# Second feed-forward matrix of a decoder block: 26 block products in place of 28

## The chip, the cores and the metric

One core of one Trainium2 chip runs the whole kernel. The metric is the device time of one execution in microseconds (us). The core has a matrix engine (PE, with its weight loads shown as PEld), a vector engine (DVE), an engine for activation functions (ACT), a general engine (POOL) and an engine that here only issues transfers (SP). Each engine takes its own instructions in the order in which the built program has them.

## What is computed

A decoder block on x of shape (4, 2048, 512): three layer norms, each followed by a sub-block that is added to x. The first is a linear recurrence over the four rows of the leading axis, the second is attention over 77 rows of context, and the third is a feed-forward block. Cut to what matters:

```python
x = x + recurrence(layernorm(x))
x = x + attention(layernorm(x), ctx) @ Wo.T          # softmax over 77 keys, 16 heads
h = layernorm(x) @ W_exp + b_exp                     # 512 -> 2048
h = gelu(butterfly(h, up_weights) + up_bias)
y = butterfly(h, down_weights) @ W_con + b_con       # 2048 -> 512
x = x + y + down_bias
```

A butterfly is linear, so butterfly and dense matrix are folded on the chip into one matrix, once per execution: a first matrix of 512 x 2048 and a second of 2048 x 512. All is in float32.

## The kernel before

**Units.** The 2048 positions are cut into 16 units of 128. A unit holds 128 positions of each of the four rows t. For each unit the kernel runs two programs side by side: `feed_forward` of unit u, and `front` of unit u+1 (first two sub-blocks and the third norm). `front` is a generator with some 50 stopping points. `feed_forward` calls `step()` after a fixed number of matmuls, and `step()` advances `front` in proportion. This gives the program order; a scheduler then sets the order on each engine from its own estimates of durations, and that order is fixed in the built program.

**Prologue.** Before the first unit, `_prepare` folds the two matrices on the chip and writes them to DRAM together with the sums of blocks that the fast products need: `up7` for the first matrix, `dn7` for the second. The front of unit 0 is mixed into it. The prologue's large buffers `wup` and `wdn` give their room to the buffers of the main loop.

**Fast block products.** Both matrices are applied by Winograd's form of Strassen's scheme: two by two blocks with seven products in place of eight. For the second matrix the left side is the activations (rows t in two halves, hidden features in two halves) and the right side is the matrix (hidden features in two halves, output features in two halves). Counted in blocks a quarter as long (one row t, a quarter of the hidden features), the seven products are 28.

**First matrix (up phase), L665.** Hidden features are taken in eight pairs p of 128. A pair has seven up products of two matmuls each, spread over `up_head(p)`, `up_tail(p-1)` and `up_mid(p)`; each matmul is 128x128 by 128x256. The right sides are blocks of the normed x (`xnt`) and four sums of them, `tb`, made by `combine` (L633 to L636). The results pass from PSUM through DVE and ACT's gelu (L670) into activations a11, a12, a21, a22 of each pair. The last gelu of the last pair, in `up_tail(7)`, makes a21. POOL then makes two sums per pair (L711, L712).

**Second matrix (down phase), L736.** `down(i)` takes seven products of 16 matmuls, one load of 1 MiB each (`w_dn`, in three rotating buffers shared with `w_up`). POOL changes the sums s of all eight pairs twice between them (L746, L753). Results are added into the residual `xt` by DVE, and by POOL for the sum u2d that goes to three places (L755).

**What stands in `front` meanwhile.** For each row t: scores on PE (L562), maximum and subtraction on DVE (L566, L567), exponential on ACT (L568), sum and reciprocal on DVE (L570, L571), the multiplication by the reciprocal on POOL (L572, 128x1232), then transposes on PE (L584), copies to SBUF by ACT and DVE (L587, L589) and the context products (L594). ACT loads a table whenever it changes between exponential and gelu. After the four rows come the output product (L504 with `ps_w`), the sums `sw` on POOL and DVE (L603 to L606), three additions on POOL (L617), and the third norm (statistics L425 on DVE, rows L451, transposes L460).

Of the kernel before, what the change touches and what calls it, by code (L numbers as in the profile page):

```python
# [23 lines left out]
NB = HID // P  # L24
NU = B // P
HC = D + 1
LOW = 7
HIGH = 4
LN_EPS = 1e-5
MAGIC = 12582912.0  # L30


# [192 lines left out]
def _prepare(nc, keep, pool, room, late, banks, dram, ident, wexp_t, up_low, up_high, up_bias, dn_low, dn_high, wcon,  # L225
             wup, wdn, bias, up7, dn7):

# [122 lines left out]
    for c in range(NC):  # L350
        for g in range(4):
# [5 lines left out]
            yield  # L357
    h = NB // 2
    order = [r * h + b for b in range(h) for r in range(2)]

    def turned(b):
        ps = banks()
        for c in range(NC):
            nc.tensor.transpose(ps[:, c * P : (c + 1) * P], wup[:, c, b * P : (b + 1) * P], ident)
        evict(t[:, b, :], ps)

    share[0] = 6
    for n in range(2):
        turned(order[n])
    for n, b in enumerate(order):  # L370
        if n + 2 < NB:
            turned(order[n + 2])
        ps = banks()
        nc.tensor.matmul(ps, lhsT=el[:, b, :], rhs=t[:, b, :], start=True, stop=True)
        evict(wdn[:, b, :], ps)
        if n == h:
            nc.sync.dma_start(out=b1, in_=brow[1, :].rearrange("(b p) -> p b", p=P))
        if n % 4 == 3:
            f = slice(n // 4 * 2, n // 4 * 2 + 2)
            b11, b12, b21, b22 = (wdn[:, r * h + f.start : r * h + f.stop, c * (D // 2) : (c + 1) * (D // 2)]  # L380
                                  for r in range(2) for c in range(2))
            t1, t2, t3, n4 = (wup[:, i, :].rearrange("p (x y) -> p x y", x=2)[:, :, f.start * P : f.stop * P] for i in range(4))
            nc.vector.tensor_tensor(t1, b12, b11, ALU.subtract)
            nc.gpsimd.tensor_tensor(t3, b22, b12, ALU.subtract)
            nc.vector.tensor_tensor(t2, b22, t1, ALU.subtract)
            nc.gpsimd.tensor_tensor(n4, b21, t2, ALU.subtract)
            for i, w in ((0, b11), (1, b21), (2, b22), (4, t1), (6, t3), (5, t2), (3, n4)):
                nc.sync.dma_start(out=dn7[i][:, f, :], in_=w)
        yield
# [5 lines left out]
def kernel(ctx: ExitStack, tc: tile.TileContext, x, ctx_t, ssm_vec, ssm_vt, ssm_vinv, wq_t, wk_t, wv_t,  # L395
# [231 lines left out]
    def combine(xnt, res):  # L627


        b11, b12, b21, b22 = (xnt[:, c : c + 2, t : t + 2, :] for c in (0, 2) for t in (0, 2))  # L630
        tb = ffn.tile([P, 4, 2, 2, P], F32, tag="tb", bufs=1, name="tb")
        t1, t2, t3, n4 = (tb[:, i] for i in range(4))
        nc.vector.tensor_tensor(t1, b12, b11, ALU.subtract)  # L633
        nc.gpsimd.tensor_tensor(t3, b22, b12, ALU.subtract)
        nc.vector.tensor_tensor(t2, b22, t1, ALU.subtract)
        nc.gpsimd.tensor_tensor(n4, b21, t2, ALU.subtract)  # L636
        res.append((b11, b21, b22, n4, t1, t2, t3))

    def feed_forward(u, xt, rhs, other):
# [4 lines left out]


        slot = [0]
        lead = 0 if u else 8

        def step():
            slot[0] += 1  # L650
            past = slot[0] - lead
            for _ in range(max(past, 0) * 50 // (102 - lead) - max(past - 1, 0) * 50 // (102 - lead)):
                next(other, None)
# [5 lines left out]
        act = []  # L659
        live = {}  # L660

        def up(p, i, ps, first):
# [9 lines left out]
        def up_head(p):  # L672
            if early:
                w = early.pop()
            else:
                w = weights([P, 7, 2, P], "w_up")
                nc.sync.dma_start(out=w, in_=up7[p])
# [11 lines left out]
        def up_mid(p):  # L689
            w, a, b, c, p1, u2 = live[p]  # L690
            up(p, 2, a, False)
            a11, a12, a21, a22, s1 = (acts.tile([P, 2, P], F32, tag=g, name=g)
                                      for g in ("a11", "a12", "a21", "a22", "s1"))
            gelu(a11, a, p)
# [4 lines left out]
            gelu(a22, a22, h + p)  # L699
            act.append((a11, a12, a21, a22, s1))  # L700

        def up_tail(p):
            w, a, b, c, p1, u2 = live[p]
            a11, a12, a21, a22, s1 = act[p]
            up(p, 4, b, False)
            nc.vector.tensor_tensor(a12, b, p1, ALU.add)  # L706
            gelu(a12, a12, h + p)
            up(p, 3, c, False)
            nc.vector.tensor_tensor(a21, c, u2, ALU.add)
            gelu(a21, a21, p)  # L710
            nc.gpsimd.tensor_tensor(s1, a21, a22, ALU.add)  # L711
            nc.gpsimd.tensor_tensor(a21, a11, a21, ALU.subtract)  # L712
            del live[p]

        for p in range(h):
            with tc.manual_schedule(engines={mybir.EngineType.PE}) if u == 0 and p < 4 else nullcontext():
# [3 lines left out]
                up_mid(p)  # L720
            if p == 1 and u + 2 < NU:
                xts[u + 2] = load_x(u + 2)
            r, d = xt[:, p // 2, p % 2 * (D // 2) : (p % 2 + 1) * (D // 2)], slice(p % 2 * (D // 2), (p % 2 + 1) * (D // 2))
            nc.gpsimd.tensor_tensor(r, r, ybias[:, d], ALU.add)  # L724
        up_tail(h - 1)

        a, b, c, b7, a4 = (bank(g).rearrange("p (t d) -> p t d", t=2) for g in "abcba")
        lhs = {1: 0, 2: 1, 3: 4, 4: 3, 5: 4, 6: 4, 7: 2}
        r11, r12, r21, r22 = (xt[:, t : t + 2, d : d + D // 2] for t in (0, 2) for d in (0, D // 2))

        def down(i, ps, first):
            w = weights([P, h, D // 2], "w_dn")
            nc.sync.dma_start(out=w, in_=dn7[i - 1])
            for p in range(h):
                for t in range(2):
                    nc.tensor.matmul(ps[:, t, :], lhsT=act[p][lhs[i]][:, t, :], rhs=w[:, p, :],  # L736
                                     start=first and p == 0 and t == 0, stop=p == h - 1, skip_group_check=True)
                step()

        def store(t, d, r):  # L740
            nc.sync.dma_start(out=out[t : t + 2, u * P : (u + 1) * P, d : d + D // 2].rearrange("t p d -> p t d"), in_=r)

        down(5, c, True)
        nc.vector.tensor_tensor(r22, c, r22, ALU.add)
        for p in range(h):
            nc.gpsimd.tensor_tensor(act[p][4], act[p][4], act[p][0], ALU.subtract)  # L746
        down(1, a, True)
        u2 = acts.tile([P, 2, D // 2], F32, tag="u2d", bufs=1, name="u2d")
        nc.scalar.copy(u2, a)
        down(6, b, True)  # L750
        nc.vector.tensor_tensor(u2, b, u2, ALU.add)
        for p in range(h):
            nc.gpsimd.tensor_tensor(act[p][4], act[p][1], act[p][4], ALU.subtract)  # L753
        for r in (r12, r22, r21):
            nc.gpsimd.tensor_tensor(r, r, u2, ALU.add)  # L755
        down(2, a, False)
        nc.vector.tensor_tensor(r11, a, r11, ALU.add)
        store(0, 0, r11)
        down(7, b7, True)
        nc.vector.tensor_tensor(r22, b7, r22, ALU.add)  # L760
        store(2, D // 2, r22)
        nc.vector.tensor_tensor(r21, b7, r21, ALU.add)
        down(4, a4, True)
        nc.vector.tensor_tensor(r21, a4, r21, ALU.add)
        store(2, 0, r21)
        down(3, c, False)
        nc.vector.tensor_tensor(r12, c, r12, ALU.add)
        store(0, D // 2, r12)
        for _ in other:
# [10 lines left out]
    wq7 = dram.tile([P, 7, NC // 2, D // 2], F32, name="wq7")  # L780
    dn7 = [dram.tile([P, NB // 2, D // 2], F32, name=f"dn7_{i}") for i in range(7)]
    xts = {}
# [3 lines left out]
    with ExitStack() as stack, tc.manual_schedule(engines={E.PE, E.SP, E.Pool}):  # L786
# [6 lines left out]
        prep = _prepare(nc, tc.keep_in_program_order, pool, rooms, lambda: xpool.tile([P, NB, P], F32, tag="xt1", name="bd"),  # L793
                        banks, dram, ident, wexp_t, up_low, up_high, up_bias, dn_low, dn_high, wcon, wup, wdn, hbias, up7, dn7)
        room = (work.tile([P, NC, T * NK], F32, tag="pr", name="ct"), xpool.tile([P, NC, D], F32, tag="xt1", name="wk"),
# [34 lines left out]
        for n, _ in enumerate(prep):  # L830
# [8 lines left out]
            if n == 24:  # L839
                xts[1] = load_x(1)  # L840
            if n == 17:
                early.append(work.tile([P, 7, 2, P], F32, tag="pt", bufs=1, name="w_first"))
# [7 lines left out]
    xlast = ctx.enter_context(tc.tile_pool(name="xlast", bufs=1, reuse_waits="tile"))  # L850
    acts = ctx.enter_context(tc.tile_pool(name="acts", bufs=NB // 2, reuse_waits="tile"))
    wts = [ctx.enter_context(tc.tile_pool(name=f"wts{i}", bufs=1, reuse_waits="tile")) for i in range(2)]
# [4 lines left out]
    def weights(shape, name):  # L857
        loaded[0] += 1
        return wts[loaded[0] % 3 - 2].tile(shape, F32, tag="w", name=name)

    combine(ready[0][2], ready)
    for u in range(NU):
# [73 lines left out]
```

## Time and profile before

| what | us |
|---|---|
| median of 3 runs | 2628.69 (2628.46 to 2633.15) |
| the profiled execution's own time | 2630.88 |
| its span | 2629.1 |
| second matrix on PE, L736, four groups of the page's table | 373.7 + 248.6 + 125.0 + 113.3 busy |
| first matrix on PE, L665, larger groups | 395.5 + 261.9 + 131.7 + 130.4 busy |
| POOL: small sums of activations L711, L712, L746, L753 | 93.1 + 98.1 + 92.9 + 97.3 |
| POOL: normalisation L572, 64 times | 143.9, 2249 ns each |
| one table load on ACT | 1283 ns, 122 of them in the two groups |
| load of w_dn, 1 MiB, from issue to landing | 4.8 (median) |

A page's line of a group gives the source line, the engine, the operation, the tiles out and in, how many, the busy time and the mean of one; after the bar stands the idle time of the engine before it and what ended it. Matmuls in float32 appear as two records each. Durations of matmuls overlap, so the price of one is read from the distance of starts.

### The profile page before, as it was taken

How to read it: one execution, taken by the hardware profiler on the slowest of the kernel's cores; microseconds unless marked ns; L12 is line 12 of the kernel's file. 1: busy time of each engine (PE TensorE's matmuls, PEld its weight loads, DVE VectorE, ACT ScalarE, POOL GpSimd, SP SyncE). 2: the span in 40 equal slices, each digit the busy share in tenths (PEclk: the TensorE clock that was granted, in tenths of full speed). 3: DMA queues.
4: the chain of work that ended last, by engine and by line, in shares of the span. 5: the costliest groups of instructions: out<-in, count | busy, mean ns of one | idle time of the engine just before them, and what ended most of it. 6: DMA issues, size and time to landing. Idle time of an engine off the chain costs nothing.

```text
span 2629.1 us, 37413 instructions
## 1 busy us (share of the span) xinstructions
PE 2565.7 (98%) x14536; PEld 2180.5 (83%) x14536; DVE 1442.7 (55%) x3333; ACT 811.4 (31%) x1472; POOL 962.0 (37%) x1045
## 2 busy tenths in 40 slices
PE   8898999999999999999999999999999999999999
PEld 5766788888888888888888888888888888888888
DVE  6665546545554654565456455645645554554541
ACT  2342414133241413324141332414124241413420
POOL 4533333415233341523435152342515234252523
PEclk9998999999999999999999999999999999999999
DMA  5735233342423334252332424233242424323243
GB/s 178 255 94 201 81 127 126 105 148 82 173 95 120 133 102 150 82 174 94 121 132 92 147 95 166 90 134 132 87 150 97 160 93 136 132 87 135 96 134 139
DMA packets 95106, 333.60 MB, mean 127 GB/s; under 512 B 15313, under 2 KB 49233, under 8 KB 77777
## 3 DMA queue, kind: packets, MB, share of 16 engines
q1 hardware_dynamic: 94930, 331.21, 36.2%
q8 instruction: 116, 1.90, 0.3%
q14 instruction: 60, 0.49, 0.1%
HBM read 297.61 MB, written 33.57 MB: 126 GB/s over the span
## 4 chain that ended last, share of the span: by engine, by line
PE 86%; DVE 7%; ACT 4%; issue 1%; POOL 1%; DMA 0%; SPq 0%; ACTq 0%; DVEq 0%; POOLq 0%
PE ps_a L736 13%; PE ps_b L665 10%; PE ps_b L736 8%; PE ps_w L504 7%; PE ps_q L504 7%; PE ps_c L665 7%; PE ps_a L665 7%; PE ps_c L736 7%; PE ps_sc L562 5%; PE ps_pt L584 4%; PE ps_s L519 3%; PE ps_o L594 2%; PE ps_t L460 2%; ACT L568 1%; DVE st L425 1%
## 5 line engine op out<-in xcount | busy, mean ns | idle before, releaser
L665 PE MATMUL ps_b<-tb,w_up 128*128 128x256 f32 x1524 | 395.5, 380 | 0.0
L736 PE MATMUL ps_a<-w_dn,a 128*128 128x256 f32 x1536 | 373.7, 380 | 0.0
L711 POOL TENSOR_TENSOR s<-a,a 128x256 f32<-128x256 f32 x128 | 93.1, 727 | 681.9 <-ACT a L670 459.5
L665 PEld LDWEIGHTS ps_b<-tb,w_up 128*128 128x128 f32 x1524 | 286.1, 191 | 39.4
L670 ACT ACTIVATE a<-a,hbias 128x256 f32<-128x256 f32 x384 | 193.8, 508 | 404.8 <-DVE a L706 276.7
L736 PEld LDWEIGHTS ps_a<-w_dn,a 128*128 128x128 f32 x1536 | 282.4, 190 | 41.6 <-issue 2.8
L665 PE MATMUL ps_a<-xnt,w_up 128*128 128x256 f32 x1016 | 261.9, 380 | 5.5 <-DMA w_up<-up 5.5
L736 PE MATMUL ps_c<-w_dn,s 128*128 128x256 f32 x1024 | 248.6, 379 | 1.2 <-POOL s L711 1.2
L461 ACT COPY xnt<-ps_t 128x512 f32<-128x512 f32 x128 | 73.6, 588 | 515.7 <-PE ps_t L460 515.7
L572 POOL TENSOR_TENSOR pr<-pr,sm 128x1232 f32<-128x1232 f32 x64 | 143.9, 2249 | 242.4 <-DVE sm L571 232.8
L665 PEld LDWEIGHTS ps_a<-xnt,w_up 128*128 128x128 f32 x1016 | 190.1, 191 | 31.2 <-DMA w_up<-up 5.9
L736 PEld LDWEIGHTS ps_c<-w_dn,s 128*128 128x128 f32 x1024 | 188.8, 190 | 29.4 <-POOL s L711 1.6
L612 DVE TENSOR_TENSOR xt<-ps_w,xt 128x512 f32<-128x512 f32 x96 | 66.2, 689 | 212.0 <-PE ps_w L504 145.8
L724 POOL TENSOR_TENSOR xt<-xt,ybias 128x256 f32<-128x256 f32 x128 | 99.3, 810 | 223.5 <-DVE xn L451 223.5
L562 PE MATMUL ps_sc<-kbd,qt 128*128 128x308 f32 x512 | 172.8, 435 | 7.4 <-DVE pr L567 6.7
L584 PE MATMUL ps_pt<-ident,pr 128*77 128x128 f32 x1024 | 144.2, 276 | 8.7 <-DVE pt L589 3.3
L568 ACT ACTIVATE pr<-pr 128x308 f32<-128x308 f32 x256 | 111.3, 457 | 132.8 <-DVE pr L567 132.2
L584 PEld LDWEIGHTS ps_pt<-ident,pr 128*77 128x77 f32 x1024 | 117.5, 147 | 41.2 <-ACT pt L587 10.3
L504 PE MATMUL ps_q<-xnt,wq 128*128 128x256 f32 x640 | 151.1, 379 | 0.0
L504 PEld LDWEIGHTS ps_q<-xnt,wq 128*128 128x128 f32 x640 | 121.4, 190 | 16.8 <-issue 0.3
L682 ACT COPY p<-ps_a 128x256 f32<-128x256 f32 x128 | 47.7, 373 | 272.8 <-PE ps_a L665 272.8
L665 PE MATMUL ps_c<-tb,w_up 128*128 128x256 f32 x508 | 131.7, 382 | 0.0
(207 smaller groups left out, 4600.8 us busy)
## 6 DMA issues: line engine op xcount, KB each, us to landing
w_dn<-dn SPq DMA_DIRECT2D x112, 1024.0 KB, 4.8
w_up<-up SPq DMA_DIRECT2D x127, 896.0 KB, 4.5
wq<-wq SPq DMA_DIRECT2D x16, 1792.0 KB, 8.4
xt<-in_x SPq DMA_DIRECT2D x16, 1024.0 KB, 5.4
out<-xt SPq DMA_DIRECT2D x64, 256.0 KB, 4.7
wdn<-in_wexp_t SPq DMA_DIRECT2D x4, 1024.0 KB, 10.2
wdn<-in_wcon SPq DMA_DIRECT2D x4, 1024.0 KB, 5.0
up<-wo SPq DMA_DIRECT2D x8, 512.0 KB, 2.8
```

What stands on the lines that cost most here:

```text
L461: nc.scalar.copy(xnt[:, :, t, :], ps)
L504: nc.tensor.matmul(tiles[key][:, r, :], lhsT=lhs(i, r, k), rhs=rhs(i, r, k), start=key == i and r == 0 and k == 0, stop=k == 1, skip_group ...
L519: nc.tensor.matmul(ps[:, 2 * i : T, f * NS : (f + 1) * NS], lhsT=xpt[:, i, c * (P // NS) + f, :], rhs=gt[:, 0 : T - 2 * i, :], start=i == ...
L562: nc.tensor.matmul(ps[:, 0 : 4 * NK], lhsT=qt[:, g, t, :], rhs=kbd[:, t, g, :], start=True, stop=True)
L568: nc.scalar.activation(pg, pg, AF.Exp, scale=1.0 / math.sqrt(DH))
L572: nc.gpsimd.tensor_tensor(pr, pr, sm.unsqueeze(2).to_broadcast([P, NH, NK]), ALU.mult)
L584: nc.tensor.transpose(pt_ps[0:NK, j, :], pr[:, 4 * g + j, :], ident)
L665: nc.tensor.matmul(ps, lhsT=w[:, c, :], rhs=rhs[i - 1][:, c], start=first and c == 0, stop=c == 1, skip_group_check=True)
L670: nc.scalar.activation(out, x, AF.Gelu, bias=hbias[:, b : b + 1])
L711: nc.gpsimd.tensor_tensor(s1, a21, a22, ALU.add)
L724: nc.gpsimd.tensor_tensor(r, r, ybias[:, d], ALU.add)
L736: nc.tensor.matmul(ps[:, t, :], lhsT=act[p][lhs[i]][:, t, :], rhs=w[:, p, :], start=first and p == 0 and t == 0, stop=p == h - 1, skip_gro ...
```

## The change

The second matrix is applied by 26 products of blocks. The left side is 16 blocks, named a(t)(k): row t, quarter k of the hidden features. The right side is eight blocks, b(k)(d): quarter k, half d of the outputs. Each product multiplies one left block or sum of left blocks by one right block or sum of right blocks, with four matmuls, and its result is added to one to four places of the output.

```diff
+FIRST = 0, NB // 2, NB // 4, 3 * NB // 4
+SUMS = {name: (x, op, y) for name, x, op, y in (line.split() for line in """d0 a13 - a03
+e a03 - a23
+f a30 - a31
+g a32 - a31
+h a10 - a00
+i a22 - a02
+n6 d0 - a12
+n7 a11 - h
...
+l24 m24 + n8""".splitlines())}
+LEFT = "l0 a11 l2 l3 e n7 l6 n11 n8 l9 n9 a00 f l13 l14 l15 n10 n6 a21 d0 g l21 l22 l23 l24 a02".split()
+DOWN = ((11, "x", "+01"), (12, "y", "+30"), (25, "w", "+00"), (5, "x", "+00"), (16, "y", "+31"), (3, "v", "+20"),
+        (14, "x", "+10"), (15, "y", "+21"), (7, "w", "+20"), (20, "z", "+31"), (1, "x", "+11"), (18, "y", "+20"),
...
```

`SUMS` has 28 sums of left blocks, each one POOL instruction of 128x512. `LEFT` names each product's left side and `DOWN` gives the order of the products: number, PSUM sum it goes to, and places (sign, row t, half d). `_down_plan` puts the sums four products ahead of their user and gives each a place: five blocks of its own (x0 to x4), the four blocks of `tb` up to product 17, and blocks a(t)2 and a(t)3 once nothing reads them any more.

```diff
+        if not isinstance(v, int):
+            fits = [p for p in free if (p[1] not in lent or last[v][1] <= until) and (n >= early or p[1] in own)]
+            best = min(fits, key=lambda p: (p[0], p[1] not in lent))
+            free.remove(best)
+            place[v] = best[1]
```

In the plan the order on POOL after the first four sums is: a23 - a20, then g = a32 - a31, i = a22 - a02, n9 = a12 - g, and so on. In the scheduled program of a unit in the steady state POOL has after a23 - a20 and g six more sums, the third normalisation, five sums, the fourth normalisation.

In the prologue all 16 blocks are transposed first, then multiplied; after every fourth one, 17 sums and one negated sum of right blocks of 128x256 are made, ten on DVE and eight on POOL, and written by two transfers; six plain blocks are written at the end:

```diff
+            for lot in RIGHT:
...
+                for i, (name, x, op, y) in enumerate(lot):
+                    made[name] = w[:, i, :]
+                    if op == "n":
+                        nc.vector.scalar_tensor_tensor(made[name], made[x], -1.0, made[y], ALU.mult, ALU.subtract)
+                        continue
+                    engine = nc.vector if name in ("24", "5", "1", "8", "14", "2", "20", "10", "22") else nc.gpsimd
+                    engine.tensor_tensor(made[name], made[x], made[y], ALU.add if op == "+" else ALU.subtract)
+                nc.sync.dma_start(out=dn26[SLOT[lot[0][0]] : SLOT[lot[0][0]] + len(lot), :, j, :].rearrange("s p d -> p s d"), in_=w)
```

In `feed_forward` the pace of `front` is set to the new number of steps, the activations go into four buffers `quarter` that hold all rows of a quarter, four sums are made in the second half of the up phase, and the down phase follows the plan. Weights come in pairs of blocks, 512 KiB each:

```diff
-            for _ in range(max(past, 0) * 50 // (102 - lead) - max(past - 1, 0) * 50 // (102 - lead)):
+            for _ in range(max(past, 0) * 50 // (98 - lead) - max(past - 1, 0) * 50 // (98 - lead)):
...
-            nc.gpsimd.tensor_tensor(s1, a21, a22, ALU.add)
-            nc.gpsimd.tensor_tensor(a21, a11, a21, ALU.subtract)
...
+            if p >= h // 2:
+                made(*plan.pop(0)[1:])
...
+        for kind, where, *rest in plan:
+            if kind == "sum":
+                made(where, *rest)
+                continue
+            i, name, goes = DOWN[rest[0]]
+            n = rest[0] % 2
+            if not n:
+                pair = weights([P, 2, NB // 4, D // 2], "w_dn")
+            nc.sync.dma_start(out=pair[:, n], in_=dn26[SLOT[str(i)]])
...
+            ps, left = sums[name], place(where)
+            for j in range(NB // 4):
+                nc.tensor.matmul(ps, lhsT=left[:, j, :], rhs=pair[:, n, j, :], start=first and j == 0, stop=j == NB // 4 - 1,
+                                 skip_group_check=True)
+                if j % 2:
+                    step()
...
+                if to[0][0] == "+":
+                    nc.vector.tensor_tensor(r, x, r, ALU.add)
+                else:
+                    nc.vector.tensor_tensor(r, r, x, ALU.subtract)
...
+            if i == 6:
+                store(3, slice(0, D // 2))
+        store(3, slice(D // 2, D))
```

A second `w_up` block is loaded ahead in the prologue, into the room of `qt`, and in unit 0 the load of x for unit 2 moves from p = 1 to p = 6:

```diff
-            if p == 1 and u + 2 < NU:
+            if p == (1 if u else 6) and u + 2 < NU:
...
+            if n == 28:
+                early.append(work.tile([P, 7, 2, P], F32, tag="qt", bufs=1, name="w_second"))
+                nc.sync.dma_start(out=early[1], in_=up7[1])
```

## The prediction

> **What bounds the kernel now.** I read the page first: one engine is nearly full, and the chain that ended last is almost all its own.
>
> ```profile
> span 2629.1 us, 37413 instructions
> ...
> PE 2565.7 (98%) x14536; PEld 2180.5 (83%) x14536; DVE 1442.7 (55%) x3333; ACT 811.4 (31%) x1472; POOL 962.0 (37%) x1045
> ...
> PE 86%; DVE 7%; ACT 4%; issue 1%; POOL 1%; DMA 0%; SPq 0%; ACTq 0%; DVEq 0%; POOLq 0%
> ```
>
> Then the windows, cut at the end of each unit's last product. The columns are length, then busy time of PE, PEld, DVE, ACT and POOL, then clock and DMA.
>
> ```profile
> 819.44:973.45 154.01, 152.68 (x865) 130.54 (x865) 85.54 (x199) 48.41 (x88) 55.50 (x58) 1.00 0.36 122
> 973.45:1127.45 154.00, 152.67 (x865) 130.52 (x865) 85.64 (x199) 48.40 (x88) 55.52 (x58) 1.00 0.35 122
> ```
>
> A unit repeats every 154.00 us and PE is idle for 1.33 of them. So PE work taken out counts in full, and so does any new wait of PE. Last, the timelines of one unit (start, duration, engine, line): PE, then POOL, then ACT.
>
> ```profile
> 914.22 0.63 PE L584 MATMUL ps_pt<-ident,pr 128*77 128x128 f32 x4 [0.36 <-ACT a L670]
> ...
> 930.21 1.04 PE L584 MATMUL ps_pt<-ident,pr 128*77 128x128 f32 x8
> ...
> 951.94 1.89 PE L736 MATMUL ps_a<-w_dn,a 128*128 128x256 f32 x8
> 953.66 1.89 PE L504 MATMUL ps_w<-wo,sw 128*128 128x256 f32 x8
> ```
>
> ```profile
> 905.19 2.25 POOL L572 TENSOR_TENSOR pr<-pr,sm 128x1232 f32<-128x1232 f32 x1 [8.86 <-DVE sm L571]
> ...
> 923.88 2.25 POOL L572 TENSOR_TENSOR pr<-pr,sm 128x1232 f32<-128x1232 f32 x1
> ...
> 941.52 1.27 POOL L603 TENSOR_TENSOR sw<-ot 128x512 f32<-128x512 f32 x1 [1.04 <-DVE ot L596]
> 942.74 1.27 POOL L605 TENSOR_TENSOR sw<-ot 128x512 f32<-128x512 f32 x1
> ...
> 947.70 3.72 POOL L617 TENSOR_TENSOR xt<-xt,w 128x512 f32<-128x512 f32 x3
> ```
>
> ```profile
> 908.09 1.28 ACT L670 ACT_TABLE_LOAD   x1
> 909.38 0.51 ACT L670 ACTIVATE a<-a,hbias 128x256 f32<-128x256 f32 x1
> ```
>
> Prices from these. Eight PE records (four matmuls of 256 columns) take 1.73 us, so 0.432 each. A POOL sum of 128x512 follows the last after 1.22 to 1.24 us; I use 1.23. A normalisation of probabilities (L572) takes 2.25. Here its third instance ends at 926.1 and PE reads it at 930.21: 4 us in hand.
>
> [...] POOL stood 8.86 us before L572 with sums queued behind. [...] The trace shows 1.28 and the next ACTIVATE 0.01 later, no drain; I use 1.29. [...]
>
> **The change part by part.** Order of instructions in the changed program is known, so positions on PE can be added up from prices: 0.432 for a 256-column matmul, 0.52 for scores (308 columns), 0.43 for four transposes, 1.01 for sixteen context matmuls. Time zero is the unit's first up matmul. On the unit before, the same addition from the first scores to 930.21 gives 31.96 of the 33.20 seen; 0.36 is the wait shown, so switches cost 0.9 on that stretch.
>
> 1. Matmuls. 112 of the second matrix become 104: 8 x 0.432 = 3.46 us a unit, 16 units: -55.3.
>
> 2. POOL sums. Removed: 32 small ones (L711, L712, L746, L753: 0.73 to 0.78 each, 23.8 us) and three of L755 (3.8). Added: 28 x 1.27 = 35.5. POOL goes from 55.5 to about 63.4 us of 150: no average problem. The order is. The sum g (a32 - a31) needs the last gelu of the up phase. Behind it in POOL's queue stand six more sums, then the third normalisation, five sums, and the fourth.
>  - When g can start: the last up product ends on PE at 78.8, with switches 79.1. DVE has the result by 79.8, but ACT's queue first holds the gelu of a12 (done 78.3), a table load, two exponentials, a load back: 78.3 + 1.3 + 0.8 + 1.3 = 81.7, then the gelu 0.5: g starts at about 82.3.
>  - Third normalisation ends at 82.3 + 7 x 1.23 + 2.25 = 93.2. PE reaches its transposes at 90.75 + 0.7 = 91.5: it waits 1.7.
>  - Fourth ends at 82.3 + 12 x 1.23 + 2 x 2.25 = 101.6. PE's place is 96.1 + 1.1 = 97.2, so the total wait is 4.3 (taking 0.1 off for overlap of starts). Everything on PE is queued behind, down products included, though their sums are ready.
>  Not shown by the old trace; bounds: without the table loads g starts no earlier than 80.2, leaving 2.3[...]. I take 4.3, in the 15 units with a next front: +64.5.
>
> 3. Other sums. Later ones sit on blocks already read: they wait for a PE product that is four or more products before their user (l6 waits for product 17 of the order, counting from 0, and is used in 23): hidden; if not, up to 1 us.
>
> 4. First softmax. DVE now takes a maximum of the next batch row ahead of the first row's sum (L570): probabilities ready near 72.5 against PE's 71.7: 0.7 x 15 = +10.5 (bounds 0 and 1.2).
>
> 5. Evictions. Seven of 128x512 (0.63 to 0.69 us) become 25, mostly 128x256 at about 0.42: some +7 us of DVE a unit, 92 of 150. Hidden, except before the third norm: there four evictions share 7.8 us with the statistics and PE waits about 0.7 instead of 0.16: +0.55 x 15 = +8 (bounds 0 and 1.5).
>
> 6. The 0.36 wait of PE shown above goes: the bank it needed is copied in time in the new order: -5.4.
>
> 7. Weights. 7 loads of 1 MiB become 26 of half that: 13 MiB a unit, always two in flight per buffer of three. The tightest place is the end of the phase, where a pair is used up in 8 x 0.432 = 3.46 us. Two other pairs cover 6.9 us; a 1 MiB load lands after 4.8. Hidden, with 2 us in hand. SP has 20 more issues; the stores and the x load stand behind the weights as before. If that cover goes: rival C.
>
> 8. Prologue. The right sums grow from 4 to 18 half-width ones per round, in four rounds: eight on POOL, 8 x 0.8 = 6.4 us a round, so POOL ends near 183.7 + 25.6 = 209 and the first up phase's own POOL sum near 211; before, PE stood until 212.88 for w_up (5.46). Two up blocks are preloaded, so PE then has 12 up products against 5, but w_up for the third waits behind about 4.5 MB of stores, until 225 to 230. I take +5 (bounds -3 and +18).
>
> 9. The last unit has no front and no wait of item 2; it ends on a smaller eviction and store (-0.5) and pulls its weights fastest (+1): +0.5.
>
> Sum on the span: -55.3 + 64.5 + 10.5 + 8 - 5.4 + 5 + 0.5 = +27.8, so 2629.1 becomes 2656.9. The profiled execution took 2630.88, 1.8 outside the span, and the median of runs is 2.2 below it: 2656.5, say 2657.
>
> **Rivals.**
> A. POOL is never late. For: its busy share is under half, and PE has other down products to issue. Against: PE issues in order, and the twelve sums and two normalisations are 19.3 us of queue against about 18.1 of PE. Then -55.3 and +5 of prologue: 2578.
> B. The wait is there, but small. This is the main case's own sum on the other side of the line: g starts at 80.2 because ACT does the gelu before the exponentials' loads, and items 4 and 5 are nothing. Per unit -3.46 + 2.3 - 0.36 = -1.5; 15 units, the last one's -3 and the prologue: -20.5, so 2608. It decides once g starts by about 81.4, where the wait equals the 3.46.
> C. Slower still: weights. Busy DMA share gives 331.21 MB / (0.362 x 2629.1 us) = 348 GB/s at full engines, 3.0 us per MiB; but the busiest slice of the page moved only 255, or 4.1. Then a pair falls 0.65 behind in each of some 7, 4.5 less 1.9 in hand = 2.6 us a unit, on top of the main case: 2657 + 42 = 2699.
> That 26 products are not what is run is excluded: PE's order has 104 matmuls.
>
> **How the numbers follow.** Main 0.57 (own range 2634 to 2688: wait from 3.4 to 5.0, prologue from -3 to 18), A 0.14, B 0.15, C 0.14. A change under 0.2% (5.3 us) can't be told from none; 0.04 of the main and B cases lies there. So faster 0.27, same 0.04, slower 0.69. Range 2600 to 2700: A lies below it, a worse C above.
>
> **What would show it.** A third and fourth L572 that end after PE is free, a wait of 1 to 2 us and one of 2 to 3 us of PE transposes on POOL in each unit, and a unit of 155 to 156.5 us, show item 2. A unit near 150.5 with no such wait shows A. PE waiting for w_dn shows C. Units equal among themselves and a first stretch longer by over 15 us would put the loss in item 8. If ACT's gelu of the last block comes 2 us earlier than I say, B follows.

## The result: 5.7% slower, and the profile after

| | before | after |
|---|---|---|
| median, us | 2630.08 (2628.46 to 2633.15, 4 runs) | 2782.00 (2778.83 to 2783.32, 4 runs) |
| ratio, 95% interval | | 1.0574 [1.0556, 1.0593] |
| span of the profiled execution, us | 2629.1 | 2781.5 |
| up to the first up product of the second unit | 372.4 | 403.8 |
| 14 units in the steady state, mean | 153.99 | 162.90 |
| last unit | 100.8 | 97.2 |

The direction was right, the size was not: 27.8 us more were forecast, 152 came. The rows below the span are read from PE's timeline, where each unit begins with an up product `ps_a<-xnt,w_up`. They split the 152.4 us of the spans: 31.4 in the first stretch, 124.7 in the 14 units (8.9 each), 3.6 given back in the last one.

The page of the changed kernel, the lines that answer to those of before:

```profile
span 2781.5 us, 37646 instructions
...
PE 2564.9 (92%) x14280; PEld 2153.5 (77%) x14280; DVE 1610.1 (58%) x3653; ACT 840.9 (30%) x1484; POOL 1110.5 (40%) x957
...
PE 54%; DVE 19%; POOL 17%; DMA 4%; issue 3%; ACT 2%; SPq 1%; POOLq 0%; DVEq 0%; ACTq 0%
```

PE has 256 records fewer and is busy all but as long (2564.9 against 2565.7 us). In the chain that ended last PE's share fell from 86% to 54%, and POOL, which had 1%, has 17%, at 40% of its time. Then the windows of two units (length; busy time of PE, PEld, DVE, ACT, POOL; clock; DMA share; GB/s):

```profile
727.68:888.42 160.74, 150.78 (x849) 127.00 (x848) 95.31 (x216) 50.64 (x89) 63.81 (x50) 1.00 0.43 156
...
1214.17:1378.35 164.18, 153.19 (x849) 129.18 (x848) 95.29 (x216) 50.63 (x89) 63.84 (x50) 0.98 0.43 152
```

PE now stands idle for 10 to 11 us of a unit, where it was 1.33. And units of the same work differ by 3.4 us: where the clock is 1.00 PE needs 150.8 us, where it is 0.98 it needs 153.2. The timelines of the unit from 1050.67 to 1214.17 show both, PE first, then POOL (start, duration, engine, line; in brackets the idle time before it and what ended it):

```profile
1148.77 0.66 PE L684 MATMUL ps_pt<-ident,pr 128*77 128x128 f32 x4 [1.81 <-POOL pr L672]
...
1157.48 1.99 PE L684 MATMUL ps_pt<-ident,pr 128*77 128x128 f32 x8 [2.85 <-POOL pr L672]
```

```profile
1137.63 1.26 POOL L821 TENSOR_TENSOR x<-q,q 128x512 f32<-128x512 f32 x1 [3.91 <-ACT q L772]
...
1146.47 2.25 POOL L672 TENSOR_TENSOR pr<-pr,sm 128x1232 f32<-128x1232 f32 x1
...
1155.18 2.24 POOL L672 TENSOR_TENSOR pr<-pr,sm 128x1232 f32<-128x1232 f32 x1
...
1177.08 3.71 POOL L717 TENSOR_TENSOR xt<-xt,w 128x512 f32<-128x512 f32 x3
```

This is the forecast mechanism: POOL stands 3.91 us before g, which waits for the last gelu, and then runs without a gap through seven sums, the third normalisation, five sums and the fourth. PE waits 1.81 and 2.85 us for them. Two things were not forecast. After 2.85 us of idling eight transposes take 1.99 us, which take 1.04 at full clock; in the unit of 834, behind the same wait, PE's clock stays 1.00. The windows behind the wait:

```profile
833.00:837.00 4.00, 2.51 (x19) 2.14 (x20) 0.99 (x2) 0.58 (x1) 1.44 (x1) 1.00 0.16 62
...
1158.00:1162.00 4.00, 4.00 (x18) 3.73 (x18) 1.37 (x2) 0.58 (x1) 0.00 (x0) 0.50 0.02 4
```

And POOL's queue does not end with the fourth normalisation: L717, three additions of the first output product onto the rows, comes at 1177.08 behind seven more sums and the three of `sw`. (Ahead of the first of these POOL itself stood 5.60 us, for a product of PE.) In the groups of the page (busy, mean ns; idle before it and its releaser) that is the chain POOL L717, DVE L712, PE L604:

```profile
L712 DVE TENSOR_TENSOR xt<-ps_w,xt 128x512 f32<-128x512 f32 x96 | 66.0, 687 | 208.4 <-POOL xt L717 118.3
...
L604 PE MATMUL ps_w<-wo,sw 128*128 128x256 f32 x512 | 124.3, 386 | 28.1 <-DVE xt L712 23.9
```

Before, L617 kept DVE's L612 waiting too (66.2 us in 16 waits), but PE did not wait for L612; now PE waits 1.70 us at an output product in each of 14 units, for a bank that L712 frees late.

### The profile page after: what moved, and what is told of

Read it like the earlier page. It is cut to its first block, busy times and chain, and to the rows that moved or that the text cites. A ratio compares the mean times of both kernels' runs of the same rounds, so it can differ in the third digit from the quotient of the medians.

```text
span 2781.5 us, 37646 instructions
## 1 busy us (share of the span) xinstructions
PE 2564.9 (92%) x14280; PEld 2153.5 (77%) x14280; DVE 1610.1 (58%) x3653; ACT 840.9 (30%) x1484; POOL 1110.5 (40%) x957
## 4 chain that ended last, share of the span: by engine, by line
PE 54%; DVE 19%; POOL 17%; DMA 4%; issue 3%; ACT 2%; SPq 1%; POOLq 0%; DVEq 0%; ACTq 0%
PE ps_b L767 9%; PE ps_c L767 6%; PE ps_q L604 6%; PE ps_a L767 5%; PE ps_w L604 4%; POOL pr L672 4%; POOL x L821 4%; POOL tb L821 4%; PE ps_b L857 4%; PE ps_s L619 3%; POOL q L821 3%; PE ps_pt L684 3%; DMA w_up<-up 3%; PE ps_sc L662 3%; DVE st L525 3%
## 5 line engine op out<-in xcount | busy, mean ns | idle before, releaser
L772 ACT ACTIVATE q<-q,hbias 128x256 f32<-128x256 f32 x384 | 194.8, 508 | 334.7 <-DVE q L808 207.2
L821 POOL TENSOR_TENSOR x<-q 128x512 f32<-128x512 f32 x32 | 40.6, 1268 | 502.9 <-ACT q L772 502.9
L712 DVE TENSOR_TENSOR xt<-ps_w,xt 128x512 f32<-128x512 f32 x96 | 66.0, 687 | 208.4 <-POOL xt L717 118.3
L689 DVE COPY pt<-ps_pt 77x512 f32<-77x512 f32 x128 | 87.5, 684 | 144.1 <-PE ps_pt L684 143.9
L662 PE MATMUL ps_sc<-kbd,qt 128*128 128x308 f32 x512 | 161.9, 427 | 7.4 <-DVE pr L667 6.7
L604 PE MATMUL ps_q<-xnt,wq 128*128 128x256 f32 x640 | 151.1, 379 | 0.0
L821 POOL TENSOR_TENSOR q<-q,x 128x512 f32<-128x512 f32 x48 | 61.1, 1273 | 225.1 <-PE ps_a L857 223.9
L604 PE MATMUL ps_w<-wo,sw 128*128 128x256 f32 x512 | 124.3, 386 | 28.1 <-DVE xt L712 23.9
L857 PE MATMUL ps_b<-w_dn,q 128*128 128x256 f32 x640 | 148.5, 379 | 0.0
L666 DVE TENSOR_REDUCE mx<-ps_sc 128x4 f32<-128x308 f32 x256 | 119.9, 473 | 42.2 <-PE ps_sc L662 37.0
L687 ACT COPY pt<-ps_pt 77x512 f32<-77x512 f32 x128 | 74.2, 580 | 215.9 <-PE ps_pt L684 215.7
L821 POOL TENSOR_TENSOR x<-q,q 128x512 f32<-128x512 f32 x80 | 114.2, 1428 | 61.9 <-ACT q L772 55.6
L857 PE MATMUL ps_b<-w_dn,x 128*128 128x256 f32 x512 | 135.9, 384 | 0.0
```

Of the source, the lines that this page charges most:

```text
L604: nc.tensor.matmul(tiles[key][:, r, :], lhsT=lhs(i, r, k), rhs=rhs(i, r, k), start=key == i and r == 0 and k == 0, stop=k == 1, skip_group ...
L662: nc.tensor.matmul(ps[:, 0 : 4 * NK], lhsT=qt[:, g, t, :], rhs=kbd[:, t, g, :], start=True, stop=True)
L666: nc.vector.tensor_reduce(mx, sc, AX.X, ALU.max)
L689: nc.vector.tensor_copy(pt, pt_ps[0:NK])
L772: nc.scalar.activation(out, x, AF.Gelu, bias=hbias[:, b : b + 1])
L821: nc.gpsimd.tensor_tensor(place(p), place(x), place(y), ALU.add if op == "+" else ALU.subtract)
```

## The experiments

All ratios are to the kernel before, run on the same chip. A "unit" is the mean of the steady ones, read as above. The edits are given in shortened form; `...` stands for what is left out.

### 1. Is the wait paid once or twice? Work put into it

```diff
     pt_ps = psum.tile([P, 4, P], F32, tag="f", name="ps_pt")
+    for _ in range(6 if tt == T - 1 and g == 0 else 0):
+        nc.tensor.matmul(pt_ps[:, 0:2, :], lhsT=ident, rhs=wo[:, 0, 0, :], start=True, stop=True)
     for j in range(4):
         nc.tensor.transpose(pt_ps[0:NK, j, :], pr[:, 4 * g + j, :], ident)
```

> The changed kernel with six matmuls of 256 columns (6 x 0.432 = 2.6 us) put on PE ahead of the fourth batch row's probability transposes, into the bank that these then overwrite; PE's order is otherwise the same. They run in the 2.85 us in which PE stood still for POOL's fourth normalisation. Theory (an idle stretch of that length costs twice: the wait itself, and some 6 us at half clock behind it): PE is given more work and the kernel gets faster; the wait there falls under 0.5 us, the half clock behind it is gone, a unit shortens by about 3.4 us from 162.9, so 14 to 15 units x 3.4 = 48 to 51 us less, near 2732. Rival (the clock falls for a reason of its own, such as load, and not because PE stood still): no change to slower by up to 15 x 0.3 us, 2780 to 2787, and half clock in the same places.

Measured: 2755.9 us, ratio 1.0476 [1.0460, 1.0492]. With 96 more matmuls the kernel is 26 us faster. PE's timeline of this kernel at that place:

```profile
990.60 2.75 PE L682 MATMUL ps_pt<-wo,ident 128*128 128x256 f32 x12
993.61 1.10 PE L684 MATMUL ps_pt<-ident,pr 128*77 128x128 f32 x8 [0.25 <-POOL pr L672]
```

The wait of 2.85 became 2.6 us of work and 0.25 of waiting, and the eight transposes behind it take 1.10 us, not 1.99; no steady unit has half clock any more. Units take 160.3 to 161.9 (mean 161.0). So the half clock costs 1.9 us a unit (162.9 less 161.0, the filler being as long as the idling it replaced). The gain lies between the two expectations: the wait is paid twice, as the theory has it, but my 3.4 was the worst unit's, not the mean's.

### 2. Does a wait of that kind cost the same in the kernel before? (e6, e7)

```diff
     nc.gpsimd.tensor_tensor(pr, pr, sm.unsqueeze(2).to_broadcast([P, NH, NK]), ALU.mult)
+    for _ in range(2 if t == T - 1 else 0):          # e6; 3 in e7
+        nc.gpsimd.tensor_tensor(pr, pr, one.unsqueeze(2).to_broadcast([P, NH, NK]), ALU.mult)
```

> The kernel before, with two more passes of POOL over the fourth batch row's probabilities (times one), 4.4 us. Its fourth normalisation ends some 3.3 us ahead of PE's need, so PE should wait 1.1 us there. Theory (a short wait costs itself and little more): 15 x 1.1 to 1.3 = 17 to 20 us more, 2647 to 2650, clock 1.00. Rival (any wait brings the half clock): 15 x 3.3 = 50 more, near 2680.

> The kernel before, with three such passes, 6.6 us: PE should wait 2.9 us there, as in the changed kernel. Theory (a wait of that length brings half clock for up to 6.5 us behind it, some 2.2 us a unit as in the changed kernel): 15 x (2.9 + 0.15 + 2.2) = 79 more, 2700 to 2715, and half clock behind the wait in most units. Rival (the half clock belongs to something else in the changed kernel, such as its higher transfer load): 15 x 3.05 = 46 more, near 2676, clock 1.00.

Measured: 2681.1 (1.0190 [1.0175, 1.0205]) and 2735.4 (1.0399 [1.0383, 1.0414]). Both are over what I expected, since the slack was smaller than I had read (in the profile of before the fourth normalisation ends at 934.81 and PE takes it up at 936.70, 1.9 us and not 3.3) and a pass takes 2.3 us: PE waited 2.64 and 4.53 us. With the wait of 4.53 the half clock came in every unit, as the theory has it. A wait of 2.64 makes units of 156.87 in twelve cases of fourteen, 0.23 more than itself; in the other two 1.2 us come on top. A wait of 4.53 makes all fourteen 160.2 to 160.9, 1.7 to 2.4 more than itself. PE's timeline and a window behind the wait in the kernel with three passes:

```profile
978.57 1.99 PE L584 MATMUL ps_pt<-ident,pr 128*77 128x128 f32 x8 [4.53 <-POOL pr L572]
```

```profile
1139.00:1143.00 4.00, 3.79 (x19) 3.52 (x20) 1.34 (x2) 0.58 (x1) 0.88 (x2) 0.61 0.00 0
```

So the half clock belongs to the idling, not to the new kernel's larger transfers. It followed 2.64 us of it in two units of fourteen (e6), 2.85 us in twelve (the changed kernel) and 4.53 us in all fourteen (e7). Its length alone does not separate these cases, though: in e2 below, 2.05 us were enough in eleven units. The times of the clock's changes tell more. In the trace of the kernel before there are 9 changes, in that of the changed kernel 39, and in each of the two traces they lie whole multiples of 3.4133 us apart, to 0.005 us over 2.6 and 2.8 ms. Here are two units of e6 cut into stretches of that length at the times of its changes, each at its wait of 2.64, and then one of e2 at its wait of 2.05 (length; PE's busy time and records; clock; DMA share; GB/s):

```profile
481.85:485.26 3.41, 1.10 (x6) 1.00 0.36 91
485.26:488.67 3.41, 3.08 (x13) 0.50 0.51 216
638.86:642.27 3.41, 2.26 (x10) 1.00 0.12 19
642.27:645.69 3.42, 1.93 (x14) 1.00 0.72 287
645.69:649.10 3.41, 3.41 (x47) 1.00 0.03 7
```

```profile
1164.28:1167.69 3.41, 1.35 (x9) 1.00 0.74 285
1167.69:1171.10 3.41, 3.41 (x12) 0.50 0.00 0
```

In the first unit of e6 PE idles for 2.31 us inside one stretch, and the next one has half clock. In the second the same wait is split between two stretches, 1.15 and 1.49 us, and nothing follows. In e2 a wait of 2.05 lies in one stretch whole, and half clock follows. The steady units of the kernels before and after, cut in this way, give counts. Of the changed kernel's stretches at full clock, 7 have 2.12 to 2.64 us of idling, and all 7 were followed by one at half clock; of the 31 with 1.45 to 1.98 us, 5 were; of the 608 with less, none, and none of the 630 of the kernel before, which have at most 0.97 us each. (The ends of matmuls are modelled in the trace, so the limits are rough.) A wait of 4.53, cut once by this spacing, leaves at least 2.26 us on one side, and half clock followed in all fourteen units of e7; the wait of 2.64 in e6 was followed in the unit where 2.31 of it fell into one stretch and not in the one where it was split.

### 3. What stands ahead in POOL's queue (e2)

```diff
-    nc.gpsimd.tensor_tensor(pr, pr, sm.unsqueeze(2).to_broadcast([P, NH, NK]), ALU.mult)
+    tc.keep_in_program_order(nc.gpsimd.tensor_tensor(pr, pr, sm.unsqueeze(2).to_broadcast([P, NH, NK]), ALU.mult))
...
-    nc.gpsimd.tensor_tensor(place(p), place(x), place(y), ALU.add if op == "+" else ALU.subtract)
+    tc.keep_in_program_order(nc.gpsimd.tensor_tensor(place(p), place(x), place(y), ALU.add if op == "+" else ALU.subtract))
```

> The changed kernel with POOL's normalisations and left sums kept in the order of the program text: the fourth normalisation then stands behind three sums after the third and not behind twelve; POOL's work is the same. Theory (what stands ahead in POOL's queue makes the three waits of 0.88, 1.81 and 2.85 us and the half clock behind the last): these go, 5.5 + 3.4 = 8.9 us a unit, 15 units, 133 us less, near 2649. Rival 1 (waits go, but the clock falls for its own reason): 15 x 5.5 = 83 less, near 2699. Rival 2 (POOL is short of throughput in that stretch, so the sums that are put back are late in turn and PE's products of the second matrix wait for them): within 20 us of 2782, with new waits of PE on POOL's sums.

Measured: 2690.6 (1.0228 [1.0213, 1.0243]), 91 us less than the changed kernel with PE's order and POOL's work unchanged; a unit takes 156.70 (most of them 156.93). The third row's wait is gone, the fourth's is 0.40, and the 1.70 at the output product is gone too, since L717 comes earlier. The first row's 0.88 stays: its normalisation has no sum ahead of it. Between the theory and rival 1, because a new loss appeared: the wait before the third norm grew from 1.03 to 2.05 us, and its window from 1167 to 1171 has a clock of 0.59; this half clock stands in eleven of the fourteen units. That is the next experiment.

### 4. The wait before the third norm (e5)

```diff
     plan = _down_plan(4, 4, own, lent, 17)
+    for n, w in ((43, "a21"), (51, "a21"), (48, "a11"), (53, "a11")):    # 43, 48: sums; 51, 53: their users
+        plan[n] = plan[n][:1] + (w,) + plan[n][2:]
```

> e2_kept with two left sums laid elsewhere: the 44th entry of the plan goes to a21 and not to a03, the 49th to a11 and not to x1, so the first of them need not wait for a product of PE (6.10 us in e2_kept) and is done before the statistics of the third normalisation end; PE's and DVE's order is the same. Theory (PE's wait of 2.05 us there, and the half clock behind it, come from POOL's two late sums: beside them DVE's small operations of two SBUF inputs take 0.5 to 1.2 us and not 0.16): the wait falls to at most 1.0 us, the half clock goes, a unit falls from 156.93 to some 154.0 to 154.8, 15 units, 32 to 44 us less than e2_kept, 2647 to 2659. Rival (DVE is simply full of the evictions of 26 products there): the wait stays at 1.7 to 2.1, 2685 to 2692.

Measured: 2653.0 (1.0085 [1.0070, 1.0100]), 37.6 us less than e2. The wait is 0.26, the clock 1.00, a unit takes 154.14 (most of them 154.20). A new wait of up to 0.92 us for a POOL sum stands at the end of the units. DVE's timeline of e2 and then of e5 at the same point of the statistics (operations on four elements a partition; x2 is two instructions in one line):

```profile
1163.45 0.99 DVE L538 SCALAR_TENSOR_TENSOR y<-w,y 128x4 f32<-128x4 f32 x2
1164.39 1.26 DVE L536 TENSOR_TENSOR w<-y,v 128x4 f32<-128x4 f32 x2
1165.62 0.24 DVE L537 TENSOR_TENSOR w<-w,y 128x4 f32<-128x4 f32 x2
```

```profile
1153.84 0.22 DVE L538 SCALAR_TENSOR_TENSOR y<-w,y 128x4 f32<-128x4 f32 x2
1154.03 0.23 DVE L536 TENSOR_TENSOR w<-y,v 128x4 f32<-128x4 f32 x2
```

In e2 POOL's two late sums ran from 1163.07 to 1165.56; the pairs beside them take 0.99 and 1.26, the third, behind them, 0.24. The profile of before has a pair of sums that are both long side by side: POOL's L634 at 980.64 takes 1.80 us and DVE's L635, from 981.35 on, 1.64; in the changed kernel the sum of L635 (L734 there) takes 0.69 at 220.12, while POOL is idle. I had not allowed for it in this stretch. In the changed kernel one such sum, at 1197.66, does it, as read from the trace: L538 at 1198.04 takes 0.99, and PE waits 1.03. The rival, that DVE is full of evictions there, is out: e5 has the same evictions in the same order.

### 5. The additions L717 (e3)

```diff
     for r in (r12, r22, r21):
-        nc.gpsimd.tensor_tensor(r, r, w1, ALU.add)
+        nc.vector.tensor_tensor(r, r, w1, ALU.add)
```

> The changed kernel with the three additions of the first output product onto the rows (L717, 3.71 us on POOL) on DVE. Theory (the wait of 1.70 us a unit at an output product, for a bank that DVE's L712 frees late because L712 needs L717's row, comes from L717 standing late in POOL's queue): the wait goes, 14 x 1.7 = 24 us less, near 2758. Rival (DVE, which then has three additions more just there, is late itself, or the wait is for another eviction): 2775 to 2790, a wait of at least 1 us at the same place.

Measured: 2749.5 (1.0454 [1.0438, 1.0469]), 32.5 us less than the changed kernel with the same order on PE. The wait at L604 for L712 is gone, and a unit takes 160.6: 2.3 less for a wait of 1.70. Most of the rest is the half clock: over the fourteen units it stands for 51 us in place of 68, which at e1's price (1.9 us a unit for those 68) is an estimated 0.5 us a unit. No run separates it.

### 6. The first stretch (e4, e8, e9)

PE's longest wait of the changed kernel, from PE's timeline:

```profile
220.86 2.07 PE L767 MATMUL ps_b<-tb,w_first 128*128 128x256 f32 x4 [15.85 <-DVE tb L734]
```

The first unit's own operands stand on DVE behind the right sums of the second matrix. From 203 to 218 us DVE is busy 14.90 of 15 us and POOL 14.37. The first experiment leaves the sums out:

```diff
     for i, (name, x, op, y) in enumerate(lot):
         made[name] = w[:, i, :]
+        continue
```

> The changed kernel with the sums of right-hand blocks of the second matrix left out (L480, L483; the stores send what lies in their buffers, so the products of the second matrix are of other numbers); all transfers stay. Theory (the first unit is 31.4 us longer, not the 5 expected, because DVE and POOL are both full in the stretch in which these sums are made): 20 to 30 us less, 2752 to 2762, all of it before the second unit starts, and the wait of 15.85 us near 221 falls under 6. Rival (the transfers fill the DMA queues there, 0.95 to 0.98 busy from 200 to 230): within 8 us of 2782, the wait near 221 still over 10.

Measured: 2759.7 (1.0487 [1.0470, 1.0505]). The second unit starts at 382.5 in place of 403.8, and the units themselves are unchanged. But the wait did not just go: 15.85 fell to 1.11, and the next one, for buffers that the stores were still reading, rose from 5.74 to 10.28. Then the sums on one engine:

```diff
-    engine = nc.vector if name in ("24", "5", "1", "8", "14", "2", "20", "10", "22") else nc.gpsimd
+    engine = nc.vector
```

> The changed kernel with all 72 right sums of the first stretch on DVE, eight of each round's eighteen taken from POOL. Theory (DVE's sums of two SBUF inputs take 0.94 us beside POOL's and 0.38 alone, so POOL's share buys nothing): the round takes 18 x 0.38 = 6.8 us, about what it takes now, and DVE no longer waits for POOL's sums (3.58 and 1.30 us): 2 to 10 us less, 2772 to 2780. Rival (two engines do the sums in parallel): eight more at 0.9 us in four rounds, 29 us more, near 2811.

Measured: 2779.8 (1.0568 [1.0541, 1.0596]); the second unit starts at 400.6, 3.2 earlier. DVE's timeline of the changed kernel, then of this one:

```profile
208.43 0.94 DVE L483 TENSOR_TENSOR wup<-wup 128x256 f32<-128x256 f32 x1
209.30 0.94 DVE L483 TENSOR_TENSOR wup<-wdn,wup 128x256 f32<-128x256 f32 x1
```

```profile
188.94 0.41 DVE L483 TENSOR_TENSOR wup<-wup 128x256 f32<-128x256 f32 x1
189.27 0.41 DVE L483 TENSOR_TENSOR wup<-wdn 128x256 f32<-128x256 f32 x1
```

Starts are 0.87 us apart beside POOL and 0.33 without it. In 0.87 us two engines make two sums, one engine alone 2.6: POOL's share of these sums was worth nothing. The whole kernel is no slower with them all on DVE, where the rival had 29 us more; whether it is faster can't be told, since its four runs spread from 2774.6 to 2789.0. Last, six stores moved ahead of two on SP:

```diff
+    if n == NB - 1:
+        for b in PLAIN:
...
     if n % 4 == 3:
...
-    if n == NB - 1:
-        for b in PLAIN:
```

> The changed kernel with the six stores of unsummed right blocks issued ahead of the last round's two lots of sums instead of behind them on SP. Theory (PE's second wait of the first stretch, 5.74 us near 235, is for these stores, whose buffer the first unit's activations take over; they stood behind lots that wait for the sums until 218): the wait falls to 0 to 3 us, 3 to 6 us less, 2776 to 2779. Rival (the queues are full from 200 to 230 whatever the order): within 2 us of 2782, the wait unchanged or moved to the next load.

Measured: 2776.8 (1.0561 [1.0532, 1.0591]), inside the theory's range and yet not for its reason: the wait of 5.74 went, one of 6.96 for w_up came, and the second unit starts at 406.2, no earlier than before the edit. The rival is right in that the wait moved to the next load. The 5 us are no gain that can be told: the four runs spread from 2772.9 to 2788.0, and in the profiled one what is less lies in the units (162.24 in the mean), whose half clock differs.

### 7. A version that might beat both (e10, e11), and what it still lacks (e12)

```diff
+    plan[46:46] = plan[47:49]; del plan[49:51]       # with e5's places, and the edits of e8 and e9
...
-    evict(wdn[:, b, :], ps)
+    nc.scalar.copy(wdn[:, b, :], ps)
```

> e5_kept_places with the 48th and 49th entries of the plan emitted before the 47th (their sums then run ahead of the next unit's eight bias additions on POOL), and in the first stretch: right sums all on DVE as in e8, the stores as in e9, the evictions of the last matmuls before the first unit on ACT alone. Theory: the wait of 0.91 us a unit for a POOL sum goes (15 x 0.91 = 14 less), the first stretch gets 5 to 15 us shorter: 2653 - 14 - 10 = 2629, 2622 to 2636, about level with the kernel before. Rival (the wait moves to the next late thing in its unit, the first stretch is bound by its transfers): 2645 to 2653.

Measured: 2641.3 (1.0040 [1.0024, 1.0055]), between the two. Seven of the fourteen units take less than the 154.00 of before (five of them 153.7); the mean is 154.13, since PE waits up to 1.08 us for w_up in others. The wait for a POOL sum is gone, but two more sums now lie beside the statistics, and the wait before the third norm is back at 0.93. This time the operation that is held up has one input only: L532 takes 0.81 us at 1140.68, beside the second sum, 0.15 in e5 (1151.74). The second unit starts at 389.6.

```diff
-    tc.keep_in_program_order(nc.gpsimd.tensor_tensor(pr, pr, sm.unsqueeze(2).to_broadcast([P, NH, NK]), ALU.mult))
+    (nc.vector.tensor_tensor if t == 0 else on_pool)(pr, pr, sm.unsqueeze(2).to_broadcast([P, NH, NK]), ALU.mult)
```

> e10_best_a with the first batch row's normalisation on DVE in place of POOL; PE's order of products between the batch rows moves with it. Theory (the first row's wait of 0.88 us is the last stage of a chain of DVE, ACT and POOL that gets 0.9 us shorter): 15 x 0.8 = 12 less than e10_best_a. Rival (DVE's longer queue or the new order on PE costs as much elsewhere): within 6 us of e10_best_a, or slower.

Measured: 2668.5 (1.0139 [1.0124, 1.0154]), 27 us slower than e10: PE's order of products moved with the edit, and PE then waits 1.03 and 0.46 us for sums, 1.04 in place of 0.40 for the fourth normalisation and 1.46 in place of 0.93 before the third norm. The first row's wait of 0.88, which the edit was for, is gone. The rival holds.

```diff
-    nc.sync.dma_start(out=dn26[SLOT[lot[0][0]] : SLOT[lot[0][0]] + len(lot), :, j, :].rearrange("s p d -> p s d"), in_=w)
...
-    nc.sync.dma_start(out=pair[:, n], in_=dn26[SLOT[str(i)]])
+    nc.sync.dma_start(out=pair[:, n], in_=dn26[18 + SLOT[str(i)] % 6])
```

> e10_best_a with the eight stores of summed right blocks (9.4 MB) left out; the products of the second matrix load the six unsummed blocks in their place, so all later transfers stay as large but the products are of other numbers. The sums themselves stay. Theory (what is left of the longer first stretch, 389.6 against 372.4 at the start of the second unit, is the time of the larger stores: 9.4 MB at 349 GB/s, 27 us, less what the old kernel stored, and the load that PE awaits for 8.98 us stands behind them on SP): that wait falls under 2 us, the second unit starts at 374 to 382, 8 to 15 us less than e10_best_a, 2626 to 2633. Rival (the sums decide, PE's wait of 10.61 us for the first unit's own operands behind them on DVE): less than 4 us saved, 2637 to 2643.

Measured: 2628.8 (0.9990 [0.9981, 0.9999]). PE's timeline of e10 and what became of it here: of

```profile
236.09 2.05 PE L767 MATMUL ps_a<-xnt,w_up 128*128 128x256 f32 x4 [8.98 <-DMA w_up<-up]
```

nothing is left, PE has that product at 223.40, and the second unit starts at 373.4, 1 us from where it started before the change. So what e10 still pays in the first stretch, 16.2 us, goes with the 9.4 MB of stores, and a kernel that computes everything and beats the one before was not found: e10 is the best, 0.4% slower.

## Why the prediction was wrong

The terms of the sum, for one steady unit (before: 154.00; forecast 155.7; measured 162.90):

| step | forecast | measured |
|---|---|---|
| 1. matmuls | -3.46 | -1.89 |
| 2. third and fourth normalisation | +4.3 | +4.66 |
| half clock behind it | none | +1.9 |
| L717 late, bank at the output product | none | +1.70 |
| 4. first softmax | +0.7 | +0.88 |
| 5. before the two norms | +0.55 | +1.19 |
| 6. the 0.36 goes | -0.36 | -0.36 |
| other waits (tq 0.39, w_up 0.5) | none | +0.9 |
| sum | +1.73 | +9.0 (8.90 seen) |

**Item 2, the queue, was right in place and size.** Seven sums, a normalisation, five sums, a normalisation: 1.7 and 2.6 were worked out, 1.81 and 2.85 measured, and e2 takes them away by order alone. What failed is what the step left out at its two ends. "Everything on PE is queued behind" was priced as the wait and no more, but PE came out of 2.85 us of idling at half clock in twelve units of fourteen, 1.9 us a unit in the mean (e1, e7). The profile of before had it: behind PE's waits of 3.77 and 5.46 us in the first stretch its windows from 201 to 205 and from 213 to 217 show clocks of 0.50 and 0.51. Shorter idling was enough in the steady units: 2.12 us within a stretch of 3.41 in the changed kernel, 2.05 in e2. The walk along POOL's queue also stopped at the fourth normalisation. It had to go on to L717, which stood seven sums further back and which DVE, and through DVE a bank of PE, waited for: 1.70 us a unit (e3).

**Item 1.** Eight matmuls a unit are gone, 3.46 us, but PE's busy time at full clock fell only from 152.67 to 150.78. In PE's timeline a change between transposes and products costs 0.07 to 0.16 us and a wait 0.15 to 0.26 beyond itself, and the new order has more of both (eight waits a unit in place of two). In e10, with five or six waits, PE is busy 150.20. This is read off the timelines, and no run was made for it alone.

**Item 3** held in the changed kernel; with other orders the sums are late by about 1 us (0.91 in e5, 1.03 in e11), the upper bound given there.

**Item 4** was right. **Item 5** had the place and half the size, and the wrong reason: not the evictions but one POOL sum beside DVE's small two-input operations (e5). That is 1.03 of the 1.19; the other 0.17, before the second norm, and the 0.39 at tq were not looked into.

**Item 7** was right: PE never waits for w_dn, and rival C is out. The last unit gave back 3.6 (forecast 3.0).

**Item 8** was the second failure: +5 with bounds of -3 and +18 against about 22 us. (31.4 in the first stretch, less the 8.9 that unit 0 loses as the others do. Leaving out the sums takes 21.3 away in e4; leaving out the stores takes 16.2 from e10's in e12.) The step priced POOL's eight sums a round at 0.8 and did not ask what DVE's ten cost beside them, 0.87 each, nor what stood behind these on DVE: the first unit's own operands. It saw the larger stores, "w_up for the third waits ... until 225 to 230", and that is the second limit, which shows as soon as the sums are gone (e4, e12).

Of the 124 us that were missed, the 14 units make 100 and the first stretch with its unit 25. By the terms of the table, times 14, the half clock is 27, L717 24, PE's switches 22, tq and w_up 13, the two norms 9, items 2 and 4 together 8.

## What to carry to other kernels

When work is added to an engine that is half idle, follow its queue past the first waiter to the last instruction that somebody needs, and then price each wait of the matrix engine with its restart: here waits of 2.85 us cost 1.9 us more than themselves in the mean of the units, and filling them with useless matmuls made the kernel 26 us faster (e1). Two engines are not always two: here DVE and POOL together made two-input sums no faster than DVE alone (two in 0.87 us, against one in 0.33 in e8), and pairs of four-element operations on DVE took 0.99 and 1.26 us in e2, beside two sums of POOL that ran 2.49 us together. A one-time stretch of a few units' length needs the same walk as the loop: every queue, what stands behind it, and the bytes.

## What the runs showed of the hardware that was not expected

- PE's clock fell to half behind 2.05 us of idling in 11 units of e2, behind 2.64 us in 2 of the 14 of e6, behind 2.85 us in 12 of the changed kernel's 14, behind 4.53 us in all 14 of e7. In the traces of the kernels before and after its changes lie whole multiples of 3.4133 us apart; of the changed kernel's stretches between such times, half clock followed all 7 with 2.12 us of idling or more, 5 of the 31 with 1.45 to 1.98 us, and none of the 608 with less.
- DVE's sums of 128x256 from two SBUF operands start every 0.33 us in e8, where POOL makes none, and every 0.87 us beside POOL's in the changed kernel; pairs of 128x4 operations took 0.23 us in e5, and 0.99 and 1.26 us beside POOL's sums of 128x512 in e2; one single-input operation of 128x4 took 0.15 us in e5 and 0.81 in e10.
